# Context queries of five pairs of units as a two-by-two block product with seven multiplications

## The chip, the cores and the metric

The kernel runs on one core of a Trainium2 chip. The core has TensorE (PE, matrix products, with its weight loads listed as PEld), VectorE (DVE), ScalarE (ACT), GpSimd (POOL) and SyncE (SP, which here issues most DMA transfers); each works through its own queue in order and waits on semaphores that the others raise. The metric is the device time of one execution in microseconds (us).

## The reference

A transformer block in float32 on x of 2 x 1024 x 256, with 16 heads of 64: self-attention, cross-attention to a context of 2 x 154 x 192, and a gated feed-forward part, each behind a layer norm and added to x. What matters here is the query of the cross-attention:

```python
q = (xq @ wq).reshape(B, S, N_HEADS, D_HEAD)     # xq = layernorm(x, ln2), 1024 x 256; wq 256 x 1024
k = (xkv @ wk).reshape(B, T, N_HEADS, D_HEAD)
v = (xkv @ wv).reshape(B, T, N_HEADS, D_HEAD)
attn = jnp.einsum('bihd,bjhd->bhij', q, k) * scale
attn = jax.nn.softmax(attn, axis=-1)
out = jnp.einsum('bhij,bjhd->bihd', attn, v).reshape(B, S, D_ATTN)
```

## The kernel before

The program is written out in the order in which each engine shall work; no scheduler reorders it. Work is cut into 16 *units*: a batch of two and a pair of heads of eight (`units`), so that a unit's query is 128 features by 1024 tokens. After the self-attention the cross-attention goes through 48 *slots* `c`, three a unit (`ui, n = divmod(c, 3)`), of three, three and two token tiles of 128. In a slot, `cross_first` issues the scores (`sc`, L873) on TensorE and their maximum (`neg`, L879) on VectorE; then ScalarE takes exponentials (L890), VectorE a reciprocal (`rden`, L898), GpSimd the scaling (L901), VectorE a slot later two transposes (`pT_ca`, L917), and once a unit is complete eight DMAs on SP's queue regroup the result (L934). `cross_weigh` in slot `n == 1` then multiplies it with the values of the unit two before: two halves of 24 matmuls (`poc`, L953), each in two PSUM banks that VectorE copies out (L967).

What remains of a slot on TensorE is filled with other pieces: the query projection of the next unit (`cross_queries`, L369, one a unit at `n == 0`), context values for every second unit (`pv_ca`, L833), output pieces of the attention (`py_ca`, `py_sa`, L500, added to x on VectorE, L507) and transposes of the next layer norm. A piece returns what has to be done with its result, and that *store* is issued in the next slot, after that slot's scores and maximum (`flush(stores)`). PSUM has eight banks of 128 x 512 float32: four hold scores (two slots deep), two are handed out in turn as `mm` (`mm_tile`) and two as `sum` (`sum_tile`). A bank can be written again once its store has read it.

The normed x is held with 64 features on the partitions: half r of the partitions has tokens r x 512 to r x 512 + 511, four chunks of 64 features. A projection multiplies four chunks with two feature halves for two token halves: 16 products of 64 x 64 by 512 columns, each done as two matmul instructions in float32 (so the trace has 32), four at a time in the four quadrants of the array, into two `mm` banks.

## Time and profile before

| | us |
|---|---|
| median of three runs (1070.14 to 1072.0) | 1070.24 |
| profiled execution | 1071.75 |
| its span, first to last instruction | 1069.1 |
| busy: PE, DVE, POOL, ACT | 1057.3, 882.9, 774.8, 645.3 |
| granted TensorE clock | 1.000 |

A line of the profile has the engine, the line of the program, what is written and read, the shapes and a count; in a timeline the first two numbers are the start and the length in us from the span's start, and brackets hold how long the engine sat idle before it and what ended that. A matmul's end is modelled, so pieces are best compared by their starts.

### The profile page before, as it was taken

How to read it: one execution, taken by the hardware profiler on the slowest of the kernel's cores; microseconds unless marked ns; L12 is line 12 of the kernel's file. 1: busy time of each engine (PE TensorE's matmuls, PEld its weight loads, DVE VectorE, ACT ScalarE, POOL GpSimd, SP SyncE). 2: the span in 40 equal slices, each digit the busy share in tenths (PEclk: the TensorE clock that was granted, in tenths of full speed). 3: DMA queues.
4: the chain of work that ended last, by engine and by line, in shares of the span. 5: the costliest groups of instructions: out<-in, count | busy, mean ns of one | idle time of the engine just before them, and what ended most of it. 6: DMA issues, size and time to landing. Idle time of an engine off the chain costs nothing.

```text
span 1069.1 us, 48669 instructions
## 1 busy us (share of the span) xinstructions
PE 1057.3 (99%) x20228; PEld 709.8 (66%) x20228; DVE 882.9 (83%) x1321; ACT 645.3 (60%) x2096; POOL 774.8 (72%) x1652
## 2 busy tenths in 40 slices
PE   8999999999999999999999999999999999999998
PEld 6556756655555556657655655576866667788998
DVE  5789999998989989999999899978877887654554
ACT  5766667677666666666777676665666554342221
POOL 2677777778777777777777777676767876499984
PEclk9999999999999999999999999999999999999999
DMA  4132122021021121111102101126776545000000
GB/s 102 38 73 54 29 68 53 25 63 41 22 52 33 34 51 33 40 34 34 45 14 54 44 14 38 33 56 145 173 177 176 123 98 119 11 11 11 21 10 30
DMA packets 86046, 60.95 MB, mean 57 GB/s; under 512 B 32123, under 2 KB 74563, under 8 KB 85827
## 3 DMA queue, kind: packets, MB, share of 16 engines
q1 hardware_dynamic: 84450, 57.07, 22.0%
q8 instruction: 159, 2.61, 1.0%
q10 hardware_dynamic: 1376, 0.79, 0.2%
q14 instruction: 61, 0.49, 0.2%
HBM read 27.91 MB, written 2.10 MB: 28 GB/s over the span
## 4 chain that ended last, share of the span: by engine, by line
PE 92%; DVE 2%; DMA 2%; POOL 2%; SPq 1%; ACT 1%; issue 1%; DVEq 0%; POOLq 0%
PE po L578 20%; PE s L526 20%; PE py_ca L500 5%; PE py_sa L500 5%; PE pk_sa L369 5%; PE pq_sa L369 5%; PE pq_ca L369 5%; PE pv_sa L405 4%; PE poc L953 4%; PE pb L1074 4%; PE pq L1219 4%; PE sc L873 3%; PE pa L1074 2%; PE pc L1074 2%; PE pf L1249 1%; PE ph_ln L286 1%
## 5 line engine op out<-in xcount | busy, mean ns | idle before, releaser
L650 POOL TENSOR_SCALAR p<-p,rd,ee 128x512 f32<-128x512 f32 x512 | 390.4, 768 | 90.4 <-DVE rd L640 89.4
L537 ACT ACTIVATE p<-s,st 128x512 f32<-128x512 f32 x512 | 345.0, 686 | 175.6 <-DVE st L712 172.4
L712 DVE TENSOR_REDUCE st<-s 128x2 f32<-128x1024 f32 x256 | 308.9, 1207 | 59.6 <-issue 20.3
L675 DVE STREAM_TRANSPOSE pT<-p 128x1024 f32<-128x1024 f32 x256 | 302.8, 1220 | 2.1 <-POOL p L650 1.9
L526 PE MATMUL s<-k_sa,q_sa 64*32 64x512 f32 x4096 | 260.3, 591 | 0.8 <-DVE k_sa L390 0.6
L578 PE MATMUL po<-pT,held_v 64*32 64x256 f32 x8192 | 241.9, 376 | 0.4 <-DMA held_v<-held_v 0.4
L578 PEld LDWEIGHTS po<-pT,held_v 64*32 64x32 f32 x8192 | 177.3, 106 | 72.5 <-issue 25.2
L526 PEld LDWEIGHTS s<-k_sa,q_sa 64*32 64x32 f32 x4096 | 90.4, 106 | 91.6 <-issue 48.1
L890 ACT ACTIVATE p<-sc,neg 128x154 f32<-128x154 f32 x256 | 96.1, 404 | 76.1 <-DVE rden L898 73.3
L901 POOL TENSOR_SCALAR p<-p,rden 128x154 f32<-128x154 f32 x256 | 96.8, 399 | 49.2 <-DVE rden L898 49.0
L537 ACT ACTIVATION_READ_ACCUMULATOR p<-s,st 128x1 f32 x512 | 104.1, 203 | 0.0
L555 POOL TENSOR_TENSOR dd<-st 128x8 f32<-128x8 f32 x128 | 25.5, 199 | 71.9 <-DMA st<-st 68.5
L500 PE MATMUL py_ca<-ca_wo,o_ca 128*128 128x256 f32 x256 | 60.2, 383 | 0.0
L369 PE MATMUL pq_ca<-hT_ln,ca_wq 64*64 64x512 f32 (+1 forms) x576 | 59.4, 589 | 0.5 <-DMA ca_wq<-in_L_xattn_ca_wq_dram 0.5
L500 PE MATMUL py_sa<-sa_wo,o_sa 128*128 128x256 f32 x256 | 59.5, 386 | 0.0
L500 PEld LDWEIGHTS py_sa<-sa_wo,o_sa 128*128 128x128 f32 x256 | 47.3, 190 | 18.0 <-issue 5.0
L369 PE MATMUL pk_sa<-hT_ln,sa_wk 64*32 64x512 f32 x960 | 57.6, 590 | 0.4 <-ACT q_sa L384 0.4
L369 PE MATMUL pq_sa<-hT_ln,sa_wq 64*32 64x512 f32 (+1 forms) x976 | 57.7, 586 | 0.0
L879 DVE TENSOR_REDUCE neg<-sc 128x6 f32<-128x924 f32 (+1 forms) x48 | 47.8, 996 | 12.0 <-PE sc L873 11.8
L890 ACT ACTIVATION_READ_ACCUMULATOR p<-sc,neg 128x1 f32 x256 | 56.5, 221 | 0.0
L405 PE MATMUL pv_sa<-sa_wv,hT_ln 64*32 64x256 f32 x1792 | 53.7, 376 | 0.0
L917 DVE STREAM_TRANSPOSE pT_ca<-p 128x480 f32<-128x480 f32 (+1 forms) x96 | 52.9, 587 | 0.8 <-POOL p L901 0.8
(158 smaller groups left out, 1479.0 us busy)
## 6 DMA issues: line engine op xcount, KB each, us to landing
wf<-pT_ca SPq DMA_DIRECT2D x128, 128.0 KB, 2.4
st<-st SPq DMA_DIRECT2D x512, 1.0 KB, 1.8
held_v<-held_v SPq DMA_DIRECT2D x32, 256.0 KB, 4.1
sa_wq<-in_L_xattn_sa_wq_dram SPq DMA_DIRECT2D x32, 128.0 KB, 2.9
sa_wk<-in_L_xattn_sa_wk_dram SPq DMA_DIRECT2D x32, 128.0 KB, 3.2
sa_wv<-in_L_xattn_sa_wv_dram SPq DMA_DIRECT2D x16, 256.0 KB, 4.5
ca_wq<-in_L_xattn_ca_wq_dram SPq DMA_DIRECT2D x32, 128.0 KB, 3.8
wf<-in_L_xattn_ff_w_dram SPq DMA_DIRECT2D x12, 256.0 KB, 3.4
```

The source lines that it names most:

```text
L369: nc.tensor.matmul(pq[r][f:f + m, at:at + n], lhsT=wt[own, c, f:f + m], rhs=h[own, c, t0:t0 + n], start=(c == 0), stop=(c == NH - 1), tile ...
L405: nc.tensor.matmul(pv[r][f:f + KB, e * VC:(e + 1) * VC], lhsT=h[half, c, t0:t0 + KB], rhs=wt[half, c, :], start=(c == 0), stop=(c == NH - ...
L500: nc.tensor.matmul(py[:, e * D:(e + 1) * D], lhsT=o[:, i, (t + e) * P:(t + e + 1) * P], rhs=wo[kind][:, g * HP + i, :], start=(i == 0), st ...
L526: nc.tensor.matmul(sc[a4 * KB:(a4 + 1) * KB, j, :], lhsT=q[r, c:c + KB], rhs=k[r, h * HB:(h + 1) * HB], start=True, stop=True, tile_positi ...
L537: nc.scalar.activation(pr[:, j, :], sc[:, j, :], AF.Exp, bias=st[:, 0, 0, i, j:j + 1], accum_out=st[:, 0, 1, i, j:j + 1],)
L578: nc.tensor.matmul(po[a2][d:d + KB, :QH // 2], lhsT=v[e][r, t, d:d + KB], rhs=pT[r, d // DH * NK + n, :], start=(t == 0 and e == 0), stop= ...
L650: nc.gpsimd.tensor_scalar(pr[:, j, :], pr[:, j, :], own["rd"][:, c:c + 1], own["ee"][:, 0, c:c + 1], op0=ALU.mult, op1=ALU.mult,)
L675: nc.vector.transpose(halves[h][:, :, c:c + KB], slots[p]["p"][i].rearrange("p j (n k) -> p (j n) k", k=KB))
L712: nc.vector.tensor_reduce(st[:, 0, 0, i, :], sc[i], AX.X, ALU.max, negate=True)
L890: nc.scalar.activation(pr_[:, j, i, :T], sc[:, j, i * T:(i + 1) * T], AF.Exp, bias=neg[:, j, i:i + 1], accum_out=den[:, j, i:i + 1],)
L901: nc.gpsimd.tensor_scalar(pr_[:, j, i, :T], pr_[:, j, i, :T], rden[:, j, i:i + 1], 1.0, op0=ALU.mult, op1=ALU.mult,)
L1074: nc.tensor.matmul(into[:, :BT], lhsT=lhs, rhs=wh[pair][i], start=first, stop=True, skip_group_check=True)
```

## The change

The queries of units 4 and 5, 6 and 7, 10 and 11, 12 and 13, 14 and 15 are computed as pairs. The rows of the block product are two quarters of the tokens (256 columns of each half), its inner dimension two halves of the features, its columns the two units. Seven products of 256 columns (`product` in `query_step`) take the place of eight. The sums of token blocks (`token_blocks`, once a batch) and of weight blocks (`weight_blocks`, for each pair) are GpSimd instructions; the sums of results are taken in PSUM where two products follow each other in a bank, and by VectorE (`plus`) elsewhere. ScalarE copies (`copy`).

A pair's products are issued in four steps, in the slots `n == 0`, `1`, `2` of one unit and `n == 0` of the next, for the pair two units ahead. Two `mm` banks (`pq`) stay with them over all four; from step 2 on they hold two `sum` banks (`pr`) also. Step 1 stands between the two halves of the context product, which both go to the `sum` banks in that slot. Units 8 and 9 keep the plain projection, in slots 20 and 21. The weights of a pair are loaded together, four DMAs in slot `n == 1` of an odd unit. Output pieces and context values move to other slots and banks accordingly, and the loads of the output weights to the front of their list.

```diff
--- before.py
+++ after.py
...
@@ -773,8 +773,136 @@
     CA = len(CG) * NU
     crossed, pTc = {}, {}
-    def cross_queries(b, pr, m=HR, bank=mm_tile, tag="QT"):
-        q = qk["ca", b, pr] = p2.tile([P, S], F32, tag=tag, name=f"q_ca{b}_{pr}")
+    def query_tile(b, pr):
+
+        u = b * NPAIR + pr
+        if u >= 4 and u % 3 == 2:
+            q = held_v[:, 3].rearrange("p t d -> p (t d)")
+        else:
+            tag = "KT" if u in (1, 3) else "QT"
+            q = p2.tile([P, S], F32, tag=tag, name=f"q_ca{b}_{pr}")
+        qk["ca", b, pr] = q
+        return q
+
+    PAIRED = (2, 4, 8, 10, 12)
+    PLAIN = {NPAIR - 1: NPAIR + 1}
+    NHH, QT4 = NH // 2, S // 4
+    block, blocks = {}, {}
+
+    def quarters(b):
+
+        h = hT["ca", b]
+        return [[h[:, c * NHH:(c + 1) * NHH, t * QT4:(t + 1) * QT4] for c in range(2)]
+                for t in range(2)]
+
+    def token_blocks(b, step):
+
+        (a11, a12), (a21, a22) = quarters(b)
+        if not block:
+            own = load_free("ck", "s1_ca", NHH * QT4)
+            block[1] = own.rearrange("p (c t) -> p c t", c=NHH)
+            own = held_v[:, 2].rearrange("p t d -> p (t d)").rearrange(
+                "p (s c t) -> p s c t", s=2, c=NHH)
+            block[2], block[4] = own[:, 0], own[:, 1]
+        tt = nc.gpsimd.tensor_tensor
+        if step == 0:
+            tt(block[1], a21, a22, ALU.add)
+        elif step == 1:
+            tt(a21, a11, a21, ALU.subtract)
+        elif step == 2:
+            tt(block[2], block[1], a11, ALU.subtract)
+        else:
+            tt(block[4], a12, block[2], ALU.subtract)
+
+    def load_free(tag, name, n):
+        return wpool.tile([P, n], F32, tag=tag, name=name)
+
+    def weight_blocks(u, step):
+
+        (b11, b21), (b12, b22) = (
+            [wsl["ca", units[u + j][1], "q"][:, c * NHH:(c + 1) * NHH, :] for c in range(2)]
+            for j in range(2))
+        t2, t3 = (pTc["spare"][:, i] for i in range(2))
+        tt = nc.gpsimd.tensor_tensor
+        if step == 0:
+            tt(t3, b22, b12, ALU.subtract)
+            tt(b12, b12, b11, ALU.subtract)
+            tt(t2, b22, b12, ALU.subtract)
+        else:
+            tt(b21, b21, t2, ALU.subtract)
+
+    def query_step(u, step):
+
+        b = units[u][0]
+        (a11, a12), (a21, a22) = quarters(b)
+        (b11, b21), (b12, b22) = (
+            [wsl["ca", units[u + j][1], "q"][:, c * NHH:(c + 1) * NHH, :] for c in range(2)]
+            for j in range(2))
+        t2, t3 = (pTc["spare"][:, i] for i in range(2))
+        if step == 0:
+            blocks["pq"] = two_banks(f"pq_ca_{u}")
+        elif step == 2:
+            blocks["pr"] = [sum_tile(f"pr_ca_{u}_{r}") for r in range(2)]
+        pq, pr = blocks["pq"], blocks.get("pr")
+
+        def product(wt, h, into, at, first):
+            for c in range(NHH):
+                for f in range(0, P, HR):
+                    for r in range(2):
+                        own = slice(r * HR, (r + 1) * HR)
+                        nc.tensor.matmul(
+                            into[r][f:f + HR, at:at + QT4], lhsT=wt[own, c, f:f + HR],
+                            rhs=h[own, c], start=(first and c == 0), stop=(c == NHH - 1),
+                            tile_position=(r * HR, f), skip_group_check=True,
+                        )
+
+        def spot(j, t, r):
+            q = qk["ca", b, units[u + j][1]]
+            return q[:, r * S // 2 + t * QT4:][:, :QT4]
+
+        def copy(bank, at, j, t):
+            for r in range(2):
+                nc.scalar.activation(spot(j, t, r), bank[r][:, at:at + QT4], AF.Copy, scale=scale)
+
+        def plus(bank, at, j, t):
+            for r in range(2):
+                own = spot(j, t, r)
+                nc.vector.scalar_tensor_tensor(
+                    own, bank[r][:, at:at + QT4], scale, own, op0=ALU.mult, op1=ALU.add)
+
+        if step == 0:
+            product(b21, a12, pq, QT4, True)
+            product(b11, a11, pq, 0, True)
+
+            def store():
+                query_tile(*units[u])
+                copy(pq, 0, 0, 0)
+                plus(pq, QT4, 0, 0)
+        elif step == 1:
+            product(t2, block[2], pq, 0, False)
+
+            def store():
+                query_tile(*units[u + 1])
+                copy(pq, 0, 1, 0)
+        elif step == 2:
+            product(b12, block[1], pr, 0, True)
+            product(t3, a21, pq, 0, False)
+
+            def store():
+                copy(pq, 0, 1, 1)
+                plus(pr, 0, 1, 1)
+        else:
+            product(b21, a22, pq, 0, False)
+            product(b22, block[4], pr, 0, False)
+
+            def store():
+                copy(pq, 0, 0, 1)
+                plus(pr, 0, 1, 0)
+
+        return store
+
+    def cross_queries(b, pr, m=HR, bank=mm_tile):
+        q = query_tile(b, pr)
         pq = [bank(f"pq_ca{b}_{pr}_{r}") for r in range(2)]
         project_both(pq, wsl["ca", pr, "q"], hT["ca", b], m)
         return lambda: take_both(q, pq, scale)
...
@@ -944,7 +1072,8 @@
         if ("ca", b, pr // HP) not in oT:
             oT["ca", b, pr // HP] = pt_.tile([P, HP, S], F32, tag="oT", name=f"o_ca{b}_{pr}")
         quarters = (a2, 2 + a2)
-        po = {a4: (mm_tile if a2 else sum_tile)(f"poc_{ui}_{a4}") for a4 in quarters}
+        bank = bank or (mm_tile if a2 else sum_tile)
+        po = {a4: bank(f"poc_{ui}_{a4}") for a4 in quarters}
         for m in range(NM + 1):
             for a4 in quarters:
                 r0 = a4 // 2 * QG
...
@@ -985,12 +1121,16 @@
         if 0 <= n < CA:
             cross_turn(n)
-    def cross_weigh(c):
+    def cross_weigh(c, between=None):
         ui, n = divmod(c - 2 * len(CG) - 1, len(CG))
         if n == 0 and 0 <= ui < NU:
-            for part in (1, 0) if pools else (0, 1):
-                run(lambda: cross_values(ui, part))
+            for i, part in enumerate((1, 0) if pools else (0, 1)):
+                run(lambda: cross_values(ui, part, sum_tile if between else None))
+                if between:
+                    flush(stores)
+                    if i == 0:
+                        held.append(between())
             flush(stores)
@@ -1366,10 +1506,13 @@
         for c in range(CA):
             if c == 1:
-                pTc["ring"] = pt_.tile(
-                    [P, 2 * NK, QH // 2], F32, tag="pT", name="pT_ca"
-                ).rearrange("p a b -> p (a b)")[:, :3 * 2 * NB * NT * KB].rearrange(
+                own = pt_.tile(
+                    [P, 2 * NK, QH // 2], F32, tag="pT", name="pT_ca").rearrange("p a b -> p (a b)")
+                n_ring = 3 * 2 * NB * NT * KB
+                pTc["ring"] = own[:, :n_ring].rearrange(
                     "p (u n j q) -> p u n j q", u=3, n=NB, j=2)
+                pTc["spare"] = own[:, n_ring:n_ring + NH * P].rearrange(
+                    "p (i c f) -> p i c f", i=2, c=NHH)
             if c == SH + 1:
                 out_pieces("sa", B - 1, NQ - 1, out_order("sa"))
             if c == SH + 1:
@@ -1382,11 +1525,13 @@
             nxt = units[ui + 1] if ui + 1 < NU else None
             if n == 0:
                 cross_beside(ui)
-            elif n == 1 and 1 <= ui < NU - 3:
-                load_weights("ca", units[ui + 3][1], "q")
-            elif n == 2 and nxt and ui:
+            if n == 1 and ui % 2 and ui < NU - 4:
+                for u in (ui + 3, ui + 4):
+                    load_weights("ca", units[u][1], "q")
+            elif n == (0 if ui % 2 else 2) and nxt and ui:
                 load_weights("ca", nxt[1], "v")
             flush(adds)
+            flush(kept)
             then = cross_first(c)
             if c < 2:
                 reciprocals(SA - 2 + c)
@@ -1409,21 +1554,42 @@
             elif c == 1:
                 run(lambda: cross_queries(*units[2]))
             elif c == 2:
-                run(lambda: cross_queries(*units[3], bank=sum_tile, tag="KT"))
+                run(lambda: cross_queries(*units[3], bank=sum_tile))
             elif c == 3:
                 run(lambda: self_values(2 * NU - 1, 0))
             elif c == 4:
                 run(lambda: self_values(2 * NU - 1, 1))
+            elif n == 0 and ui in PAIRED:
+                run(lambda: query_step(ui + 2, 0))
+                run_work(0, 1)
+                run_work(0, 0, n_sum=1)
+                run(lambda: context_values(*units[ui], bank=sum_tile))
+            elif n == 0 and ui - 1 in PAIRED:
+                run(lambda: query_step(ui + 1, 3))
+                run_work(0, 1)
             elif n == 0 and ui:
-                if nxt and ui > 2:
-                    run(lambda: cross_queries(*nxt))
+                if ui in PLAIN:
+                    run(lambda: cross_queries(*units[PLAIN[ui]]))
                 else:
                     run_work(2, 0)
                 run_work(0, 1)
+            elif n == 1 and ui in PAIRED:
+                spare["turned"] = True
+                run_work(0, 1)
+                flush(adds)
+                flush(slow)
+                cross_weigh(c, lambda: query_step(ui + 2, 1))
+                stores.extend(held)
+                held.clear()
+            elif n == 2 and ui in PAIRED:
+                run(lambda: query_step(ui + 2, 2))
+                run_work(0, ui != HP)
+                if ui == HP:
+                    load_out_weights()
             elif n == 1:
                 spare["turned"] = True
-                run_work(0, 1, sum_tile if outs else None)
+                run_work(0, 1, sum_tile)
                 flush(stores)
                 run_work(0, 0, n_sum=1)
                 if ui % 2 == 0:
@@ -1434,17 +1600,30 @@
                 flush(stores)
                 cross_weigh(c)
             elif n == 2:
-                run_work(0, ui != HP, sum_tile if ui == HP + 1 else None)
+                run_work(0, ui != HP, sum_tile if ui - 1 in PAIRED else None)
                 if c == SH + 1:
-                    run_work(2, 0)
-                elif ui == HP:
-                    wo["ca"] = const.tile([P, NPAIR, D], F32, tag="wo", name="ca_wo")
-                    later[1:1] = [lambda i=i: nc.sync.dma_start(
-                        out=wo["ca"][:, i, :], in_=w["ca_wo"][i * P:(i + 1) * P, :])
-                        for i in range(NPAIR)]
+                    run_work(2, 0, n_sum=1)
+                elif ui - 1 in PAIRED:
+                    run_work(0, 0, n_sum=1)
+                elif ui == NPAIR - 2:
+                    run(lambda: cross_queries(*units[NPAIR], bank=sum_tile))
             flush(slow)
             cross_regroup(c)
-            for _ in range(min(1 if ui in (HP, HP + 1) else 2, len(later))):
+            if c in (1, 3, 5, 6):
+                token_blocks(0, (1, 3, 5, 6).index(c))
+            elif c in (3 * NPAIR - 3, 3 * NPAIR - 2):
+                i = 2 * (c - 3 * NPAIR + 3)
+                if i == 0:
+                    token_blocks(1, 0)
+                    token_blocks(1, 2)
+                else:
+                    token_blocks(1, 1)
+                    token_blocks(1, 3)
+            if n == 2 and ui + 1 in PAIRED:
+                weight_blocks(ui + 3, 0)
+            elif n == 1 and ui in PAIRED:
+                weight_blocks(ui + 2, 1)
+            for _ in range(min(1 if ui == HP + 1 or ui == HP and n == 0 else 2, len(later))):
                 later.pop(0)()
             if c == CA - 22:
                 weighted = [fn for n in range(4) for fn in weight_sums(n)]
```

More of the change, by code (lines that the diff above doesn't have):

```diff
@@ L830, in context_values @@
         v = vs["ca", b, pr // 2] = vs["own", i % 2]
-        pv = mm_tile(f"pv_ca{b}_{pr}")
+        pv = bank(f"pv_ca{b}_{pr}")
         for c in range(2):
@@ L969, in cross_values, with load_out_weights @@
         return store
+    def load_out_weights():
+        wo["ca"] = const.tile([P, NPAIR, D], F32, tag="wo", name="ca_wo")
+        later[0:0] = [lambda i=i: nc.sync.dma_start(
+            out=wo["ca"][:, i, :], in_=w["ca_wo"][i * P:(i + 1) * P, :])
+            for i in range(NPAIR)]
     def cross_beside(ui):
```

6 lines of the change are left out of this document (3 added, 3 removed).

## The prediction

> **What bounds the kernel now.** I read the page first (span, busy time, chain), then the stretches of the cross-attention stage, then that stage's timeline, one engine at a time.
>
> ```profile
> span 1069.1 us, 48669 instructions
> ...
> PE 1057.3 (99%) x20228; PEld 709.8 (66%) x20228; DVE 882.9 (83%) x1321; ACT 645.3 (60%) x2096; POOL 774.8 (72%) x1652
> ...
> PE 92%; DVE 2%; DMA 2%; POOL 2%; SPq 1%; ACT 1%; issue 1%; DVEq 0%; POOLq 0%
> ```
>
> TensorE is 92% of the chain that ended last. The change lies in the cross-attention stage, which runs from about 700 to 897 us. Four stretches of it (length; busy us of PE, PEld, DVE, ACT, POOL; granted clock; DMA share; GB/s):
>
> ```profile
> 730.00:736.00 6.00, 4.62 (x88) 3.18 (x89) 4.55 (x14) 2.93 (x14) 3.25 (x9) 1.00 0.16 36
> 736.00:760.00 24.00, 24.00 (x338) 17.91 (x335) 22.53 (x57) 15.70 (x73) 19.00 (x52) 1.00 0.67 161
> 784.00:808.00 24.00, 24.00 (x309) 16.14 (x304) 17.32 (x35) 14.80 (x70) 14.53 (x41) 1.00 0.74 185
> 833.00:858.00 25.00, 24.63 (x320) 16.70 (x313) 22.69 (x56) 14.87 (x70) 21.64 (x55) 1.00 0.56 129
> ```
>
> A busy PE isn't yet a PE at its peak, so I take the intervals between the starts of its pieces. One unit of the steady part:
>
> ```profile
> 809.31 3.61 PE L369 MATMUL pq_ca<-hT_ln,ca_wq 64*64 64x512 f32 x32
> 812.74 0.96 PE L873 MATMUL sc<-kT,q_ca 64*64 64x154 f32 x24
> 813.63 3.72 PE L500 MATMUL py_ca<-ca_wo,o_ca 128*128 128x256 f32 x16
> 817.28 1.09 PE L953 MATMUL poc<-wf,held_v 64*64 64x256 f32 x16
> ...
> 818.63 1.04 PE L953 MATMUL poc<-wf,held_v 64*64 64x256 f32 x16
> ...
> 819.93 1.49 PE L873 MATMUL sc<-kT,q_ca 64*64 64x154 f32 x40
> 821.24 3.61 PE L369 MATMUL pq_ca<-hT_ln,ca_wq 64*64 64x512 f32 x32
> ...
> 827.39 1.03 PE L833 MATMUL pv_ca<-ca_wv,ctxT 96*128 96x256 f32 x4
> 828.26 1.89 PE L500 MATMUL py_ca<-ca_wo,o_ca 128*128 128x256 f32 x8
> 830.08 1.09 PE L953 MATMUL poc<-wf,held_v 64*64 64x256 f32 x16
> ...
> 834.03 0.61 PE L369 MATMUL pq_ca<-hT_ln,ca_wq 64*64 64x512 f32 x4
> ```
>
> Every piece starts where the one before stops issuing, so TensorE never waits here: two units take 834.03 - 809.31 = 24.7 us. The prices are: a query projection 3.43, scores of three token tiles 0.89 (of two, 1.31 - 0.89, say 0.5), a half of the context product (`poc`) 1.30, one output piece (`py`) 1.8, context values (`pv`) 0.87.
>
> **What it saves.** A projection is 32 matmuls of 512 columns, four at a time: eight groups in 3.43, 0.43 a group. A `poc` half is 24 of 256 columns: six groups in 1.30, 0.217 a group, so half-width matmuls cost half. Before, two units pay 2 x 3.43 = 6.86. After, seven products of 16 half-width matmuls, four groups each, pay 7 x 4 x 0.217 = 6.07. The saving is 0.8 us a pair, 4.0 for five pairs, if nothing waits. That is all TensorE can gain; the other queries (units 0 to 3, 8 and 9) keep their matmuls.
>
> **What it adds on other engines.** Per pair VectorE gets six added 128x256 sums out of PSUM, ScalarE eight half-width copies for four full ones, GpSimd four 128x256 sums; eight sums of 512 columns come once for the tokens.
>
> ```profile
> L1119 DVE SCALAR_TENSOR_TENSOR own<-pb,cols,own 128x256 f32<-128x256 f32 x32 | 15.5, 484 | 23.3 <-PE pb L1074 23.3
> ```
> ```profile
> L1045 POOL TENSOR_TENSOR w1s<-wf 128x256 f32<-128x256 f32 x4 | 2.9, 726 | 0.0
> ```
> ```profile
> L1183 POOL TENSOR_TENSOR quick<-wf 128x512 f32<-128x512 f32 x1 | 1.3, 1272 | 0.0
> ```
>
> (Groups of equal instructions; after the bar, busy us and mean ns of one.) VectorE: 6 x 0.48 = 2.9 us a pair. GpSimd: 4 x 0.73 = 2.9 a pair and 8 x 1.27 = 10.2 for the tokens, 25 in all. In the stretch from 784 both engines have room (17.32 + 2.9 and 14.53 + 2.9 of 24); in those from 736 and 833 VectorE has none (22.53 + 2.9, 22.69 + 2.9). As work alone I price them at nothing, because the 24 us of TensorE work beside them cover them; without that cover they cost their 2.9 a pair. The weight loads move too: two units' weights are issued together, four DMAs, every second unit. That is the same number, ahead of the eight regrouping DMAs on SP's queue, with over a slot to land before the first product: nothing.
>
> **What it adds in waits.** The order matters more. All seven products live in the two `mm` banks from step 0 to step 3, and steps 2 and 3 take both `sum` banks too. So each step writes a bank that VectorE or ScalarE must first read, and VectorE's queue in a slot is: the slot's score maximum (`neg`, which waits for that slot's scores), then the sums, a reciprocal, two transposes, then the context copies. TensorE's first piece in the slot is the scores. So nothing is freed before the scores are done and the maximum has run. The durations:
>
> ```profile
> 813.77 1.12 DVE L879 TENSOR_REDUCE neg<-sc 128x6 f32<-128x924 f32 x1 [0.68 <-PE sc L873]
> 814.81 0.18 DVE L898 RECIPROCAL rden<-den 128x6 f32<-128x6 f32 x1
> 814.90 0.87 DVE L917 STREAM_TRANSPOSE pT_ca<-p 128x320 f32<-128x320 f32 x2
> 815.69 0.67 DVE L507 TENSOR_TENSOR x<-py_ca,x 128x512 f32<-128x512 f32 x1
> ...
> 818.85 0.76 DVE L967 COPY o_ca<-poc 128x256 f32<-128x256 f32 x2 [0.76 <-PE poc L953]
> ...
> 820.81 0.79 DVE L879 TENSOR_REDUCE neg<-sc 128x4 f32<-128x616 f32 x1
> 821.52 0.18 DVE L898 RECIPROCAL rden<-den 128x6 f32<-128x6 f32 x1
> ```
> ```profile
> 812.38 0.38 ACT L890 ACTIVATE p<-sc,neg 128x154 f32<-128x154 f32 x1
> ...
> 812.75 0.39 ACT L890 ACTIVATE p<-sc,neg 128x154 f32<-128x154 f32 x1
> ```
> ```profile
> 732.88 0.76 ACT L843 COPY held_v<-pv_ca 64x256 f32<-64x256 f32 x2
> ...
> 733.69 0.86 PE L953 MATMUL poc<-wf,held_v 64*64 64x256 f32 x10 [1.38 <-ACT held_v L843]
> ```
>
> From these: a maximum 1.04 (0.71 for two tiles), sum 0.43 to the next, pair of transposes 0.79, copies 0.76, an exponential 0.37. Scores stop issuing at 813.63 and their maximum starts 0.14 later; `poc` hands over after 0.22 (818.63 to 818.85); TensorE resumes 0.05 after a release (732.88 + 0.76 to 733.69). The last row is such a wait already: a bank whose copy stood behind a slot's exponentials.
>
> I walk one steady pair by hand, zero where TensorE starts the scores of the slot with step 1.
>
> - Scores to 0.89. `pv` of the slot before ended at 0, is copied by 1.0; `poc` a goes 1.05 to 2.35 (wait 0.16).
> - Maximum 1.03 to 2.07, step 0's two sums to 2.98. Step 1 overwrites their bank: 3.03 to 3.90 (wait 0.68).
> - Reciprocal and transposes to 3.85, copies of `poc` a to 4.60. `poc` b needs the same two banks: 4.65 to 5.95 (wait 0.75).
> - `poc` b's copies end 6.93. Scores to 6.45; step 2's first product needs the banks: 6.98 to 7.85 (wait 0.53), the second to 8.7.
> - Next scores to 9.6. ScalarE copies step 2's second product only behind four exponentials (maximum done 7.6, exponentials 9.1, copies 9.85): step 3's first product 9.9 to 10.8 (wait 0.3).
> - Its second needs step 2's sums, behind that slot's maximum (9.74 to 10.78): sums done 11.65, product 11.7 to 12.6 (wait 0.9).
> - Scores to 13.5. The output piece wants the bank of step 3's sum, behind another maximum (13.6 to 14.65, first sum 15.1): wait 1.65.
>
> The waits add to 5.0 us a pair; minus the 0.8 saved, the pair loses 4.2. Five pairs: 21 us. The first pair has VectorE full besides and would lose more, but wins back waits such as the 1.38 above; I leave it at 4.2. Sum against the profiled execution's own 1071.75 (span 1069.1): 1092.8. The median of the runs, 1070.24, lies 1.5 below, so I forecast 1091.
>
> Bounds for a wait that the trace doesn't show: below, the nearest row is the steady part with no wait at all (0); above, a copy that stands behind a slot's work costs 1.38, seven times 9.7 a pair. I take 5.0, nearer the walk's rows than either end, since each of its terms is a difference of quoted durations.
>
> Why step 1 waits for a sum in the other half of its bank: in the built program its first matmul waits for that VectorE instruction, not only for the copy of the half it overwrites. The Trainium skill ("PSUM — Partial Sum Buffer", section on bank collisions) has the reason: two engines may not be in one bank and quadrant at once, whichever columns they touch, so software must guard by bank. Waiting by columns would save that 0.68, 3.4 us over five pairs, and leave a loss of 17.6; no run here shows it.
>
> **Rivals.**
>
> Gain: the waits are covered because VectorE releases each bank before TensorE comes to it. Then only the 4.0 stays: 1067.8 profiled, 1066. It decides where the seven waits together fall under 0.8 a pair. For it: the steady part has no wait though banks are handed on there too. Against it: there `py` and a 3.43 projection stand between scores and reuse; after, a 0.87 product does.
>
> Partial: half the waits are covered, 2.5 a pair, by pieces that I count as waiting for both banks where they need one at first: +1.7 x 5 = 8.5, 1079.
>
> VectorE (or GpSimd) is the bound in the full stretches, and the waits come on top: two to three pairs there carry 2.9 more each, +6 to +9: about 1098. For it: 22.69 and 21.64 busy of 25. Against: TensorE's waits stretch the stage and give both room.
>
> The clock. In the row from 730 TensorE idles 1.38 at a stretch and the granted clock stays 1.00; the paired slots hold 24 us of TensorE work a pair, so a clock at half speed for two fifths of it would add 10 a pair: 1091 + 50 = 1141. The Trainium skill ("TensorE: Matmul & The Clock Gate", on micro-idles under PSUM cycling) says frequent short idles can make the gate oscillate; the trace so far disagrees, no wait of the walk is above 1.7.
>
> That the change doesn't do what it says is excluded: the built program has seven products a pair.
>
> **How the numbers follow.** The walk 0.62, its own range 1082 to 1100; partial cover 0.16; VectorE or GpSimd on top 0.08; clock 0.02; gain 0.09; within 0.2% (2 us, about what a measurement of this kernel tells from no change) 0.03. Slower: 0.62 + 0.16 + 0.08 + 0.02 = 0.88. The range for 8 in 10 reaches from inside partial cover to VectorE on top, 1074 to 1103; it leaves out the gain, the clock and the edges.
>
> **What would show it.** Right: the paired query matmuls at 256 columns, 0.217 for four; TensorE waits on VectorE's sums (line of `scalar_tensor_tensor`) and on `o_ca` copies, some 0.5 to 1.7 each, five times each; paired units near 29 us for two instead of 24.7, units 8 and 9 unchanged. Wrong: PE back to back in paired slots, or waits put down to GpSimd or DMA. The forecast fails most likely in the size of the waits, if a release comes earlier than the slot's maximum.

## The result, and the profile after

The changed kernel takes 1102.52 us (median of 5 runs, 1100.85 to 1104.79) against 1070.24 (1070.13 to 1072.18): ratio 1.0299, 95% interval 1.028 to 1.0318. It is 32 us slower. The forecast was 1091 in a range up to 1103, so the sign and the range held, the range by half a microsecond, and 11 us are missing from the walk, whose own range ended at 1100. The profiled execution took 1104.54 with a span of 1102.6, 33.5 more than before. From the page:

```profile
span 1102.6 us, 49283 instructions
...
PE 1072.1 (97%) x20468; PEld 739.9 (67%) x20468; DVE 896.3 (81%) x1353; ACT 649.0 (59%) x2114; POOL 802.6 (73%) x1680
...
PE 82%; DVE 5%; DMA 4%; POOL 3%; SPq 2%; issue 2%; ACT 1%; POOLq 0%; DVEq 0%; ACTq 0%
```

TensorE's share of the chain falls from 92% to 82%. That is some 110 us, far more than the loss, so most of it is another path of the chain through stages that take no longer. All but 0.9 us of the loss lies in the cross-attention stage: its slot 0 starts 0.9 us later than before, its slot 47 33.8 later. A steady pair (units 12 and 13), TensorE and then VectorE, from the timeline (start, duration, engine, line, operation, count, idle before):

```profile
848.23 1.02 PE L1001 MATMUL sc<-kT,q_ca 64*64 64x154 f32 x24
849.07 1.16 PE L1082 MATMUL poc<-wf,held_v 64*64 64x256 f32 x16
...
850.91 1.33 PE L853 MATMUL pq_ca<-held_v,pT_ca 64*64 64x256 f32 x16 [0.25 <-DVE q_ca L870]
852.34 1.20 PE L1082 MATMUL poc<-wf,held_v 64*64 64x256 f32 x14
...
853.68 0.30 PE L1001 MATMUL sc<-kT,q_ca 64*64 64x154 f32 x2
...
854.38 0.43 PE L853 MATMUL pr_ca<-s_ca,ca_wq 64*64 64x256 f32 x1
...
856.16 0.29 PE L1001 MATMUL sc<-kT,held_v 64*64 64x154 f32 x1
...
857.68 1.27 PE L853 MATMUL pq_ca<-hT_ln,ca_wq 64*64 64x256 f32 x16 [0.23 <-POOL p L1029]
859.01 1.20 PE L853 MATMUL pr_ca<-held_v,ca_wq 64*64 64x256 f32 x13
859.93 0.29 PE L1001 MATMUL sc<-kT,held_v 64*64 64x154 f32 x1
...
863.04 3.69 PE L500 MATMUL py_ca<-ca_wo,o_ca 128*128 128x256 f32 x16 [1.82 <-DVE q_ca L870]
```
```profile
849.32 1.12 DVE L1007 TENSOR_REDUCE neg<-sc 128x6 f32<-128x924 f32 x1 [1.15 <-PE sc L1001]
850.35 0.75 DVE L870 SCALAR_TENSOR_TENSOR q_ca<-pq_ca,q_ca 128x256 f32<-128x256 f32 x2
...
851.11 0.86 DVE L1045 STREAM_TRANSPOSE pT_ca<-p 128x320 f32<-128x320 f32 x2
851.90 0.71 DVE L1096 COPY o_ca<-poc 128x256 f32<-128x256 f32 x2
...
861.47 1.09 DVE L1007 TENSOR_REDUCE neg<-sc 128x6 f32<-128x924 f32 x1
862.48 0.75 DVE L870 SCALAR_TENSOR_TENSOR q_ca<-pr_ca,q_ca 128x256 f32<-128x256 f32 x2
```

A piece's start less the start and price of the piece before it is its wait. Step 1 starts at 850.91, where the first context half (849.07 + 1.30) was issued at 850.37: 0.54. Its releaser is the first of the two sums at 850.35, which stands behind the maximum at 849.32. The second half waits 0.56 for the copies at 851.90, behind the transposes. The output piece starts at 863.04 where the scores were done at 860.82: 2.2, for the sum at 862.48, behind the maximum at 861.47. The wait of step 3 (857.68) is put down to GpSimd by the profile, which the prediction named as a sign of being wrong; but in all five pairs that step starts 0.14 to 0.15 behind the end of ScalarE's copy out of its bank, and it still does in experiment 8 in this pair, where the nearest GpSimd instruction ends 0.26 ahead of it. So the copy is the likelier releaser, as in the walk.

For the whole stage I cut the time at the starts of the maxima of every sixth slot, count TensorE's matmuls between and take their prices off; the rest is time for which no matmul accounts (waits, and a lowered clock). Lengths and rests in us; the last stretch ends with the start of slot 47's maximum:

| slots | steps of | length before | after | rest before | after |
|---|---|---|---|---|---|
| 6-11 | first pair | 22.7 | 31.1 | 2.4 | 10.6 |
| 12-17 | second pair | 25.2 | 29.5 | -0.4 | 5.0 |
| 18-23 | none | 25.2 | 28.4 | -0.5 | 2.4 |
| 24-29 | third pair | 24.7 | 27.7 | -0.2 | 4.8 |
| 30-35 | fourth pair | 25.9 | 29.9 | -0.3 | 5.0 |
| 36-41 | fifth pair | 24.9 | 28.9 | -0.2 | 4.8 |
| 42-46 | none | 19.8 | 24.5 | 0.1 | 6.5 |

Four pairs have a rest of 4.8 to 5.0, the walk's 5.0. The excess is elsewhere: 5.6 above that in the first stretch (which had 2.4 before the change), 2.4 and 6.5 in stretches that hold no step at all. Two places in those show another thing. Windows of the changed kernel (length; busy us of PE, PEld, DVE, ACT, POOL; granted clock; DMA share; GB/s), around slots 10 and 46:

```profile
748.00:756.00 8.00, 6.88 (x68) 4.13 (x66) 4.80 (x15) 1.63 (x10) 4.34 (x11) 0.57 0.36 85
...
921.00:928.00 7.00, 5.88 (x64) 4.76 (x65) 3.54 (x10) 1.71 (x10) 3.17 (x8) 0.76 0.55 121
```

The clock falls to half, and 8 x 0.43 + 7 x 0.24 = 5.1 us are lost to it. Ahead of each fall TensorE idles. Slot 46, TensorE and VectorE:

```profile
919.00 0.65 PE L286 MATMUL ph_ln<-ident,xn_ln 128*128 128x128 f32 x4
919.59 0.65 PE L1082 MATMUL poc<-wf,held_v 64*64 64x256 f32 x4
922.12 0.86 PE L1082 MATMUL poc<-wf,held_v 64*64 64x256 f32 x10 [1.88 <-issue]
```
```profile
919.14 1.12 DVE L1007 TENSOR_REDUCE neg<-sc 128x6 f32<-128x924 f32 x1
...
920.27 0.86 DVE L1045 STREAM_TRANSPOSE pT_ca<-p 128x320 f32<-128x320 f32 x2
921.06 0.95 DVE L297 TENSOR_SCALAR hT_ln<-ph_ln,cols 128x256 f32<-128x256 f32 x2
```

The transposes `ph_ln` take a `sum` bank right ahead of the context product, which needs both. They are copied out (L297) behind maximum and transposes, done at 922.01, and `poc` goes on at 922.12. Before the change slot 46 had no `ph_ln`, and the context product followed the scores at once:

```profile
889.07 1.02 PE L873 MATMUL sc<-kT,q_ca 64*64 64x154 f32 x24
889.90 1.04 PE L953 MATMUL poc<-wf,held_v 64*64 64x256 f32 x16
```

The change moved the output pieces of slots 19 and 43 one slot ahead and put `ph_ln` into slots 10 and 46. In these four slots nothing but values or `ph_ln` now stands between the scores and the context product. I call a piece that fills this place the slot's cover: slots 19 and 43 lost theirs, while slots 10 and 46 had none before either, but waited for no bank.

### The profile page after: what moved, and what is told of

Same layout as the page of the kernel before. It is cut to its first block, busy times and chain, and to the rows that moved or that the text cites. A ratio compares the mean times of both kernels' runs of the same rounds, so it can differ in the third digit from the quotient of the medians.

```text
span 1102.6 us, 49283 instructions
## 1 busy us (share of the span) xinstructions
PE 1072.1 (97%) x20468; PEld 739.9 (67%) x20468; DVE 896.3 (81%) x1353; ACT 649.0 (59%) x2114; POOL 802.6 (73%) x1680
## 4 chain that ended last, share of the span: by engine, by line
PE 82%; DVE 5%; DMA 4%; POOL 3%; SPq 2%; issue 2%; ACT 1%; POOLq 0%; DVEq 0%; ACTq 0%
PE s L526 17%; PE po L578 17%; PE py_ca L500 5%; PE py_sa L500 5%; PE pk_sa L369 4%; PE pq_sa L369 4%; PE poc L1082 4%; PE pv_sa L405 4%; PE pb L1214 4%; PE pq L1359 3%; PE sc L1001 3%; DMA st<-st 2%; PE pa L1214 2%; PE pc L1214 2%; SPq L547 2%
## 5 line engine op out<-in xcount | busy, mean ns | idle before, releaser
L712 DVE TENSOR_REDUCE st<-s 128x2 f32<-128x1024 f32 x256 | 308.9, 1207 | 58.1 <-issue 19.8
L578 PEld LDWEIGHTS po<-pT,held_v 64*32 64x32 f32 x8192 | 183.0, 106 | 66.0 <-issue 23.7
L526 PEld LDWEIGHTS s<-k_sa,q_sa 64*32 64x32 f32 x4096 | 93.4, 106 | 89.4 <-issue 42.7
L500 PEld LDWEIGHTS py_ca<-ca_wo,o_ca 128*128 128x128 f32 x256 | 47.1, 190 | 13.4 <-issue 6.3
L1018 ACT ACTIVATION_READ_ACCUMULATOR p<-sc,neg 128x1 f32 x256 | 53.2, 208 | 0.0
```

What stands on the lines that cost most here:

```text
L500: nc.tensor.matmul(py[:, e * D:(e + 1) * D], lhsT=o[:, i, (t + e) * P:(t + e + 1) * P], rhs=wo[kind][:, g * HP + i, :], start=(i == 0), st ...
L526: nc.tensor.matmul(sc[a4 * KB:(a4 + 1) * KB, j, :], lhsT=q[r, c:c + KB], rhs=k[r, h * HB:(h + 1) * HB], start=True, stop=True, tile_positi ...
L578: nc.tensor.matmul(po[a2][d:d + KB, :QH // 2], lhsT=v[e][r, t, d:d + KB], rhs=pT[r, d // DH * NK + n, :], start=(t == 0 and e == 0), stop= ...
L712: nc.vector.tensor_reduce(st[:, 0, 0, i, :], sc[i], AX.X, ALU.max, negate=True)
L1018: nc.scalar.activation(pr_[:, j, i, :T], sc[:, j, i * T:(i + 1) * T], AF.Exp, bias=neg[:, j, i:i + 1], accum_out=den[:, j, i:i + 1],)
```

## Experiments

Every comparison is with runs of the kernel before on the same chip (medians 1071.42, 1069.26 and 1070.50 in the three groups). All edits are to the changed kernel.

### 1. `ph_ln` behind the context product

```diff
-                run_work(0, 1, sum_tile)
+                behind = not outs
+                if not behind:
+                    run_work(0, 1, sum_tile)
...
                 cross_weigh(c)
+                if behind:
+                    run_work(0, 1, sum_tile)
```

> The change made three slots bare (10, 43, 46): no output piece is left for them, and the transposes of the normalised tokens (ph_ln) now go into a sum bank right ahead of the context product, which must wait for VectorE's copies of ph_ln. In the trace of the changed kernel that is 2.13 (ph_ln on GpSimd's xn_ln) + 1.12 us in slot 10, 1.14 in slot 43, 1.88 in slot 46, and behind them 14 us at a granted clock of 0.76 (3.4 us) and 5 us at 0.66 (1.7 us): 11.3 us in all. Here ph_ln of a slot without output pieces goes behind both halves of the context product; nothing else is moved. Theory A (this order makes the 11 us which the walk of the prediction missed): 1091 to 1095, no stretch under 0.95 of the clock around 744-758 and 922-927. Rival B (the bare slot waits in any order, for values, copies or maxima, and the clock falls all the same): over 1099. Rival C (the missing 11 us are general VectorE load): no change, 1102.

Measured: 1100.87 us, ratio 1.0276 (1.026 to 1.0291). A miss for theory A; rival B had it. TensorE and VectorE in slot 10:

```profile
743.34 1.16 PE L1001 MATMUL sc<-kT,q_ca 64*64 64x154 f32 x23
746.50 1.20 PE L1082 MATMUL poc<-wf,held_v 64*64 64x256 f32 x14 [2.00 <-issue]
```
```profile
744.98 1.09 DVE L1007 TENSOR_REDUCE neg<-sc 128x6 f32<-128x924 f32 x1
745.98 0.75 DVE L870 SCALAR_TENSOR_TENSOR held_v<-pr_ca,held_v 128x256 f32<-128x256 f32 x2
```

Without `ph_ln` in the way, the context product waits 2.00 in the same place, for step 3's sums behind the maximum: the walk's 1.65 under another name. So slot 10 is held by the sums as well as by `ph_ln`, and only what came on top went. In slot 43 a wait of 1.38 for the copied values replaces the 1.14. The clock stays up in slots 10 and 46 but falls in slots 7 and 8 (0.58 from 734 to 738), behind waits of 0.25 and 1.15, the same two that leave it at 1.00 in the changed kernel.

### 2. Sums issued in their own slot

```diff
                 run(lambda: query_step(ui + 2, 0))
+                flush(stores)
...
                 run(lambda: query_step(ui + 1, 3))
+                flush(stores)
...
-                stores.extend(held)
-                held.clear()
+                flush(held)
...
                 run(lambda: query_step(ui + 2, 2))
+                flush(stores)
```

> The copies and sums of steps 0, 2 and 3 are issued in their own slot, right behind their products, and those of step 1 at the end of its slot, so VectorE and ScalarE have them in their queues ahead of the next slot's maximum and exponentials instead of behind. Theory A (the walk: step 1 waits 0.68, step 3 0.3 and 0.9, the output piece 1.65 because the sums stand behind a maximum): of the 5.0 us of waits a pair 3.5 go, 17.5 us in all; some comes back as a later maximum, so 1085 to 1091. Rival B (the waits come from too few banks between steps, whatever the order on VectorE): under 5 us gained, over 1097. Rival C (VectorE in its order is the bound and sums ahead of the maximum delay it and the exponentials as much as they free): 1102 or more.

Measured: 1095.34 us, ratio 1.0222 (1.0205 to 1.0239): 7 gained, between A and B. Rests of the pairs: 10.5, 3.1, 2.9, 2.4, 5.1, so 1.9 to 2.6 a pair went where the walk had 3.5, and nothing in the first. The fifth shows what came back:

```profile
870.38 0.76 DVE L870 SCALAR_TENSOR_TENSOR held_v<-pq_ca,held_v 128x256 f32<-128x256 f32 x2 [1.54 <-ACT held_v L865]
...
872.20 0.66 DVE L507 TENSOR_TENSOR x<-py_ca,x 128x512 f32<-128x512 f32 x1
872.78 1.11 DVE L1007 TENSOR_REDUCE neg<-sc 128x6 f32<-128x924 f32 x1
```
```profile
872.92 2.20 PE L1082 MATMUL poc<-wf,held_v 64*64 64x256 f32 x16 [1.67 <-DVE x L507]
```

A sum adds to what ScalarE's copy has put in the query tile. Issued early, it makes VectorE stand 1.54 for a copy that is behind six exponentials, and the addition that frees the `sum` bank stands behind the sum; half clock follows from 872 to 877, 1.7 us. The waits do hang on the order on VectorE; putting the sums first only moves part of them.

### 3. Eight products, no sums

```diff
         if step == 0:
-            product(b21, a12, pq, QT4, True)
             product(b11, a11, pq, 0, True)
+            product(b21, a12, pq, 0, False)
...
                 copy(pq, 0, 0, 0)
-                plus(pq, QT4, 0, 0)
```

Likewise two plain products in each other step, each accumulating in one bank half, and no operand sums.

> The same four slots, banks and order, but the queries as eight plain half-width products (two a step) with no sums: no operand sums on GpSimd, no sums on VectorE, eight half-width copies on ScalarE as in the changed kernel. One product more a pair: +0.87 x 5 = +4.3 us of TensorE. Theory A (most of the waiting is for VectorE's sums: 0.68 + 0.9 + 1.65 a pair): the waits fall from 5.0 to about 1.8 a pair, 16 us, and the time goes to 1088 to 1093, faster than with seven products. Rival B (the waiting comes from the split into four slots that hold the two mm banks and push both context halves into the sum banks, not from the sums): 1105 to 1108.

Measured: 1087.66 us, ratio 1.0153 (1.0134 to 1.0172): faster by 15 us than seven products, as A said. All waits of its TensorE in the stage:

```profile
PE poc L1080 <- issue: 3.0, 2, 1.9
PE ph_ln L286 <- POOL xn_ln L273: 2.6, 1, 2.6
PE poc L1080 <- ACT held_v L969: 1.6, 2, 1.4
PE poc L1080 <- DVE hT_ln L297: 0.9, 1, 0.9
PE poc L1080 <- DVE o_ca L1094: 0.3, 1, 0.3
```

(Total us, times, longest.) What is left belongs to the uncovered slots. The rests of the second to fifth pair are 0.7, 1.2, 0.8 and 0.7: four slots and two shared banks cost little, and about 4 of the 5 us a pair go with the sums, over four times the 0.87 that the eighth product costs. Not all of that need be the sums' own: step 1 now has two products, so VectorE has 0.87 us more to copy the first context half, and the 0.56 of the second half may have gone by that.

### 4. No operand sums on GpSimd

```diff
-            product(t2, block[2], pq, 0, False)
+            product(b12, a21, pq, 0, False)
...
-                weight_blocks(ui + 3, 0)
```

> The operand sums on GpSimd (some 25 us of its work) are left out and the seven products read plain blocks instead, so the queries of the paired units are not the reference's; products, banks, copies and VectorE's sums stay. Theory A (they are hidden, but for a share of the first pair, where TensorE waits 2.1 for a normalised tile that GpSimd makes): 0 to 4 us, 1098 to 1102. Rival B (GpSimd, 73% busy, holds up the scaling and so transposes, regrouping and context product): 10 us or more, under 1092.

Measured: 1103.08 us, ratio 1.0298 (1.0283 to 1.0314). No gain, the lower end of A's 0 to 4 us (the time is 1.1 above its 1102): GpSimd's 25 us of added sums are hidden.

### 5. Output pieces spread again

```diff
-                    run_work(2, 0)
+                    run_work(2 if ui == NU - 1 else 1, 0)
...
-                elif ui - 1 in PAIRED:
+                elif ui - 1 in PAIRED and ui < NU - 3:
...
-                run_work(0, 1, sum_tile)
+                run_work(0, 1, sum_tile if outs or ui < NU - 1 else None)
```

> Of the changed kernel only the places of four output pieces (1.8 us of TensorE each) and of one transpose are altered, outside the paired steps: slots 18 and 19 get one piece each instead of two and none, slot 41 gives its second piece to slot 42, slot 43 has two (as before the change) instead of none, and slot 46 has no ph_ln. Theory A (what the walk missed outside the pairs is that slots 19, 43 and 46 were left without cover: TensorE's unaccounted time is 2.4 us in slots 18 to 23 and 6.5 in slots 42 to 47, of it 1.7 by a clock of 0.5 to 0.7): 6 to 8 us gained, 1094.5 to 1096.5; both stretches come to under 1.5. Rival B (these waits come from the late maxima of the slots, so a piece that is moved uncovers another wait of the same length): under 2.5 us gained.

Measured: 1096.75 us, ratio 1.0248 (1.0233 to 1.0262): 5.4 by the ratio, a little under A. The last stretch's rest goes from 6.5 to 1.5, with no fall of the clock; that of slots 18 to 23 only from 2.4 to 1.8.

### 6 and 7. Filling the gaps of slots 10 and 46

The edit of the second run; the first had eleven matmuls in each fill, at the same places.

```diff
+    def fill(c, n):
+        pd = mm_tile(f"fill_{c}")
+        for _ in range(n):
+            nc.tensor.matmul(
+                pd[:, :B * TP], lhsT=ident, rhs=kT[:, 0, :], start=True, stop=True)
...
+                if c == 10:
+                    fill(c, 3)
                 run_work(0, 1, sum_tile)
+                if c in (10, CA - 2):
+                    fill(c, 2 if c == 10 else 3)
```

> Work is only added: eleven matmuls of 192 columns into a free mm bank whose result nobody reads, some 1.8 us, twice in slot 10 (ahead of ph_ln and behind it) and once in slot 46 (behind ph_ln), where TensorE of the changed kernel stands idle for 2.13, 1.12 and 1.88 us and the granted clock then falls to 0.5 for some 6.8 and 3.4 us (3.4 and 1.7 us lost). Theory A (the idle time makes the clock fall): with the gaps filled the clock stays at 1.00 there, and the kernel is faster with 5.4 us more work: 1097.5 to 1100. Rival B (the clock falls for another reason, say the load of the stage or chance): still under 0.8 around slots 10 and 46, and 1102 to 1106. Rival C (the clock stays up but the added work delays as much as it saves): 1101 to 1104.

Measured: 1108.83 us, ratio 1.0374 (1.036 to 1.0389), clock 1.00 in both places. My fills were 6.0 us each, so this showed the clock but not the price. The second run had the sizes right:

> The run with filled gaps again, with fills of the length of the gaps. The first fills were mis-sized: the block is 320 columns wide, so each took 6.0 us instead of 1.8 (22 matmuls, 0.27 each); the clock did stay at 1.00 in slots 10 and 46, and 18 us of added work cost 6.3. Now 6 matmuls (1.6 us) ahead of ph_ln and 4 (1.1 us) behind it in slot 10, and 6 behind ph_ln in slot 46. Theory A (idle time of TensorE makes the clock fall, and the fills take only time that was idle): clock 1.00 at both places and 1097.5 to 1099.5, faster than the changed kernel with 4.4 us more work. Rival B (the clock stays up but what the fills delay costs as much): 1101.5 to 1104. Rival C (short fills don't keep it up): clock under 0.8 there.

Measured: 1098.72 us, ratio 1.0265 (1.025 to 1.028): 3.8 us faster than the changed kernel with 4.4 us more work on TensorE, as A said. The same windows, and slot 46:

```profile
748.00:756.00 8.00, 7.90 (x129) 5.68 (x126) 7.17 (x20) 2.48 (x13) 5.70 (x16) 1.00 0.60 130
...
921.00:928.00 7.00, 7.00 (x35) 6.17 (x33) 5.54 (x12) 3.25 (x10) 5.68 (x14) 1.00 0.54 116
```
```profile
915.11 1.78 PE L989 MATMUL fill<-kT,ident 128*128 128x320 f32 x6
916.82 0.65 PE L1088 MATMUL poc<-wf,held_v 64*64 64x256 f32 x4
917.73 0.86 PE L1088 MATMUL poc<-wf,held_v 64*64 64x256 f32 x10 [0.26 <-issue]
```

The context product comes no sooner against its scores, but it runs at the full clock. The slots stand earlier here, so the second window lies behind slot 46; the clock is 1.00 in 742 to 752 and in 913 to 921 too, which hold the two slots. The mean clock is 1.000 in all four executions of this run, and 0.995 to 0.998 in the five of the changed kernel. That idle time of TensorE costs clock is shown by this run.

### 8. Copies ahead of the transposes

```diff
-            cross_drain(c)
+            if n != 1 or ui not in PAIRED:
+                cross_drain(c)
...
                     flush(stores)
                     if i == 0:
+                        cross_drain(c)
                         held.append(between())
```

> One thing alone: in the slots with step 1 VectorE copies the first context half ahead of the two transposes (0.79 us) instead of behind. Theory A (the walk: the second half waits 0.75 for those copies, because they stand behind reciprocal and transposes): 0.5 to 0.75 us a pair, 2.5 to 3.7 in all, 1098.5 to 1100; TensorE's unaccounted time in a steady pair falls from 4.9 to about 4.3. Rival B (the transposes, now later, hold up the copies of the second half and so step 2 by as much): 1101.5 to 1103.

Measured: 1098.78 us, ratio 1.0265 (1.0248 to 1.0283): 3.7 gained, as A said. The rests of the second to fifth pair fall by 0.7, 0.3, 0.3 and 0.4, some 2 over five pairs with the first, so the term is nearer 0.4 than 0.75. In the profiled executions a further 1.7 is clock: slot 10 loses 1.7 us to it instead of 3.4. The rest of the gain in time isn't explained.

### 9. Without step 0's sums

```diff
                 copy(pq, 0, 0, 0)
-                plus(pq, QT4, 0, 0)
```

> The two sums of step 0 are left out (one quarter of the first unit's queries of each pair lacks a product); the product stays. Theory A (the walk: step 1 waits 0.68 for these sums, which lie in the other half of its bank, and all later work of VectorE in that slot moves up by their 0.91): step 1 starts right behind the first context half and the second half starts 0.9 us sooner: 0.7 to 0.9 a pair, 3.5 to 4.5 in all, 1098 to 1099. Rival B (step 1 is held by the copies of step 0 on ScalarE, or the second half by something else than VectorE's queue): under 1.5 us, over 1101.

Measured: 1101.10 us (1096.64 to 1102.1), ratio 1.0279 (1.0258 to 1.0301). By the time alone rival B has it (over 1101, 1.4 us gained), but 2 us are within this run's interval. The trace speaks for A's waits, in the pair shown above:

```profile
846.85 1.02 PE L1000 MATMUL sc<-kT,q_ca 64*64 64x154 f32 x24
847.68 1.16 PE L1081 MATMUL poc<-wf,held_v 64*64 64x256 f32 x16
...
848.98 1.16 PE L853 MATMUL pq_ca<-held_v,pT_ca 64*64 64x256 f32 x16
850.29 1.20 PE L1081 MATMUL poc<-wf,held_v 64*64 64x256 f32 x14
```

Step 1 starts at 848.98, right behind the first context half (wait 0 instead of 0.54), and the second half starts 0.67 sooner against its scores. But the rests of the pairs fall only by 0 to 0.8, since the last wait, for step 3's sums, keeps its 1.82.

### 10. Three pairs

```diff
-    PAIRED = (2, 4, 8, 10, 12)
-    PLAIN = {NPAIR - 1: NPAIR + 1}
+    PAIRED = (8, 10, 12)
+    PLAIN = {3: 4, 4: 5, 5: 6, 6: 7, 7: 9}
```

> Only the last three pairs (units 10 to 15) as block products; units 4 to 7 get their plain projections as before the change, each a unit ahead. Theory A (a pair costs what the walk says, 4.2, wherever it stands, and the rest is the uncovered slots): the three steady stretches of six slots cost 2.9 + 4.0 + 3.9 more than before the change, slots 18 to 23 up to 3.2 and slots 42 to 47 4.4: 1069.5 + 14 to 19 = 1084 to 1088. Rival B (the first two pairs carry most of the loss, being the ones with VectorE full): under 1081. Rival C (one pair is enough to lose the clock and the covers): over 1092.

Measured: 1099.75 us, ratio 1.027 (1.0249 to 1.029). A miss for A and B; only C has the time. The three pairs' stretches are what they were (27.7, 29.9 and 28.9), but slots 6 to 23, with no step in them, take 86.9 us: 89.0 in the changed kernel, 73.2 before the change. Two waits there:

```profile
734.24 0.86 PE L1082 MATMUL poc<-wf,held_v 64*64 64x256 f32 x10 [2.38 <-ACT held_v L971]
...
743.44 0.74 PE L286 MATMUL ph_ln<-ident,xn_ln 128*128 128x128 f32 x4 [2.16 <-POOL xn_ln L273]
```

The clock is at half from 744 to 751 once more. So this order of pieces, banks and `ph_ln` loses most of that time with plain projections too. But it has waits of its own (2.8 us of `poc` for regrouping DMAs that neither kernel shows), so it doesn't give the price of the first two pairs alone; that stays open.

### 11 and 12. All together, with seven and with eight products

The edits of experiments 5 and 8, and `ph_ln` behind the context product in slot 10; with seven products also that of experiment 2.

> Seven products with all that the runs so far point to: sums and copies issued in their own slots, the pieces of slots 18, 19 and 41 to 43 spread again, ph_ln behind the context product in slot 10 and none in slot 46, and, new, in the step-1 slots the copies of the first context half ahead of the two transposes on VectorE. Theory A (the terms add; the walk's 0.75 for the second half on the copies of the first goes too): from 1095.3 with early sums alone, 7 less for the spread pieces, 2 to 3 less for slot 10, 5 x 0.5 less for the copies: 1082 to 1085. Rival B (each wait that goes uncovers the next, VectorE's chain of maximum, sums, copies and transposes being as long as TensorE's work of the slot): over 1088. Below 1070 by no theory.

> The same order as the run above, with eight plain products and no sums. Theory A (with covers back the split into four slots costs nearly nothing, 0.85 us unaccounted a pair, and 0.87 more work than two projections' 6.86 less 0.09): from 1087.7, 7 to 8 less for the spread pieces, 2 to 3 for slot 10: 1077 to 1080; faster than seven products by 3 to 6 us. Rival B (seven products catch up once the order is good, since they have 4.3 us less work): slower than the run above.

Measured: seven products 1085.75 us, ratio 1.0153 (1.0136 to 1.017); eight 1080.37, ratio 1.01 (1.0087 to 1.0114). Both end a little over their theory A. Eight products win by 5.4 us with a product more. No version found beats the kernel before; the 4 us that seven products save on TensorE don't pay for the sums in any order tried.

## Why the prediction was right, and where it fell short

**The saving.** Right in size. The traces have 320 matmuls of 512 columns fewer and 560 of 256 more; at the prediction's prices that is 34.3 us against 30.4, so 3.9 saved where 4.0 was forecast. The price of a product holds: in experiment 3 two of them in a row take 1.73 us (840.03 to 841.76), 0.87 each.

**The walk of a steady pair.** Right: rests of 5.0, 4.8, 5.0, 4.8 for a forecast 5.0. Term by term in the pair shown, forecast and measured: context half a 0.16 and 0; step 1 0.68 and 0.54; half b 0.75 and 0.56; step 2 0.53 and some 0.3; step 3 0.3 and 0.63, then 0.9 and 0.46; the output piece 1.65 and 2.2. The sum is 4.97 against 4.7, by some luck: single terms are off by up to 0.55. Two are too long for the same reason: half b and step 3's second product start behind the first of two copies or sums (852.34, while the copies run from 851.90 to 852.61), where the walk had both. That most of it goes with the sums was argued there and is shown by experiment 3; that the order on VectorE carries them, by 2, 8 and 9. The chain is tighter than the walk had it: taking one wait away (3.5 by the walk in experiment 2, 0.75 in 8, up to 0.9 in 9) gave about half, since the next one grew.

**GpSimd at nothing.** Right, by experiment 4.

**Step 1 behind a sum in the other half of its bank.** It waits for that sum, and not at all when the sum is left out (experiment 9). This agrees with the rule of the Trainium skill ("PSUM — Partial Sum Buffer", section on bank collisions), which has software guard by bank; a version that ignores the bank wasn't tried.

**What was missed.** The step that failed is the list of the change's parts: it had products, sums, copies and loads, and took all else as unmoved ("units 8 and 9 unchanged", the first pair "at 4.2", nothing for slots 42 to 46). The change also moves output pieces ahead, so that slots 19 and 43 lose their cover, and puts `ph_ln` into a `sum` bank in the bare slots 10 and 46. In the profiled execution the rests grow by 3.2 more than walked in slots 6 to 11, by 2.9 in 18 to 23 and by 6.4 in 42 to 46. Experiment 5 won back 5.4 of it by moving four pieces and keeping `ph_ln` out of slot 46. What the first pair loses above the walk is open in part (experiment 10).

**The range.** That it held is luck. Its upper end of 1103 stood for VectorE or GpSimd as the bound in the full stretches. The fourth and fifth pair, where VectorE was full (833 to 858), show nothing on top of the walk (5.0 and 4.8), and experiment 4 clears GpSimd's sums; whether VectorE's load adds to the first pair, in the other full stretch, no run shows. The time went into the slots without cover and the clock instead, and two of the five executions lie above 1103.

**The clock.** Given 0.02 and put aside because it stayed at 1.00 behind an idle 1.38. One row with a single wait was no bound: 5.1 us of the profiled execution are lost at half clock (inside the rests just named), and experiment 7 shows the cause. This execution has the lowest mean clock of the five (0.995, the others 0.997 or 0.998), so the others lost less. The price was far from the rival's 50 us, since it falls in two places and not in every pair. The rule cited there, from the Trainium skill ("TensorE: Matmul & The Clock Gate", section on psum-queue depth-cycling), is that frequent short idles make the clock fall and rise again. The trace agrees in part: short idles cost clock in slots 10 and 46, but the steady pairs with their seven waits stay at 1.00.

**The sum.** 21 for the walk, 3.2 + 2.9 + 6.4 = 12.5 for the three stretches, 0.7 of growing rests in the other pairs and 0.9 at the stage's start make 35.1, where the span grew by 33.5. Counting by prices and stretches is no closer than that.

## What to carry to other kernels

Before you save a matmul by adding sums, look at what stands ahead of the sums on the engine that adds. Here each sum stood behind a maximum that waits for TensorE itself, and a pair without the sums, with one product more, was about 4 us shorter in waits for 0.87 us of work. When a change re-orders a tuned schedule, list every slot that loses its filler or gets a new user of its banks, also among the slots that the change doesn't name. And price TensorE's idle time twice: as the wait, and as the clock behind it; a filler that does nothing useful can then make a kernel faster.

## What the runs showed of the hardware

The granted clock fell to half for some 3 to 7 us behind a single wait of 1.88 us (slot 46) and behind 2.13 and 1.12 us with a short piece between (slot 10), and stayed at 1.00 with those gaps filled. The Trainium skill ("TensorE: Matmul & The Clock Gate", Part 1) names an idle window of about 3.4 us for the fall; no single wait here is that long, so by these runs less is enough. It is not a fixed threshold either: waits of 0.25 and 1.15 left the clock at 1.00 in the changed kernel and were followed by half clock in experiment 1, and the same wait of 1.88 in slot 46 left it at 1.00 in experiments 2, 3 and 10. What decides it is open. In every trace that has a fall it cost 1.7 or 3.4 us (4 us at a mean of 0.58 in experiment 1, 8 us at 0.57 in the changed kernel).
